# A four-layer vision stack in one kernel: one matmul a half in the chunked scan's preparation, and in the spectral layer fuller matmuls, paired row tiles and five result buffers

## The chip, the cores and the metric

The kernel runs on one core of a Trainium2 chip. The metric is device time in microseconds (us) of that core, the median over the runs. All arithmetic is in float32. A matmul of float32 operands shows in the trace as two records on TensorE (PE), each with its own weight load (PEld); a transpose shows as one. The other engines are DVE (VectorE), ACT (ScalarE), POOL (GpSimd) and SP (SyncE, which here only issues DMAs).

## The reference, cut to what matters

The input is `(8, 64, 64, 96)`: eight images of 64x64 positions and 96 channels. Four layers follow, each a residual step on a group-normed input. Layers 0 and 2 are selective scans over four directions; this change doesn't touch them. Layer 1 is a chunked scan and layer 3 a spectral layer:

```python
x = x + _L1_conv_ref(_gn(x), ...)   # chunked scan: chunks, four directions, decays by exp of sums
x = x + _L3_conv_ref(_gn(x), ...)

# layer 3
xc = jnp.transpose(x, (0, 3, 1, 2))
xu = _upsample_rfft(xc)              # 64x64 -> 128x128, low-passed
h = jnp.transpose(xu, (0, 2, 3, 1))
h = h @ W1.T + b1                    # 96 -> 384
h = coef[:, 0] + coef[:, 1] * h + coef[:, 2] * (h * h)
h = h @ W2.T + b2                    # 384 -> 96
hl = _lpf_rfft(jnp.transpose(h, (0, 3, 1, 2)), cutoff=0.5)
out = hl[:, :, ::2, ::2]             # back to 64x64
return jnp.transpose(out, (0, 2, 3, 1))
```

In layer 1 a projection `x_proj` gives, for each of four directions, 6 step sizes and two vectors of 16 numbers (B and C) at each position.

## The kernel before, in words

The eight images are worked one after the other in a Python loop (`for b in range(batch)`), all unrolled. Within an image each layer is a stage of its own: group norm, `project`, the scan, `back`; the spectral layer closes the image. Where a block says `tc.manual_schedule()` the order of instructions is the one written; elsewhere, and so in both places of this change, a planner orders the instructions of each engine ahead of time by its own costs, and each engine's queue then runs strictly in that order.

**Chunked scan.** `chunked_scan` calls `chunked_order` twice, for `o = 0` (positions by rows) and `o = 1` (by columns), each for two directions `k = o + 2 * i`. The preparation is the first block of `chunked_order`. For `o = 0` it also holds the 3x3 convolution, mostly on DVE (L258), with `silu` on ACT (L272). Then the PE makes B and C for whole rows (`pr`, L782), which DVE copies (`bcs`, L790) and SP sends to DRAM (`bcd`, L793). The loop `for c in range(NQ)` goes over 32 chunks of 128 positions. Each chunk needs its tokens transposed (`xt`, positions on partitions, 192 channels in two halves of 96) and its step sizes and B (`xd`, 2 directions x 22 numbers). For `o = 1` POOL (L802) and ACT (L803) first copy the chunk into rows (`uc`, four buffers). Then come two transposes into `pt` (L807), one copy to `xt` by DVE or ACT in turn (L808), and two matmuls that sum into `px` (L812). `px` takes four chunks and DVE copies it once for the four (L820). After the loop come the step sizes (`dt`, L824, L829), the decays (L834 to L841) and the second block, with its order written by hand, whose first loads (`bt`, `cr`, L863, L867) read `bcd`.

**Spectral layer.** `spectral_layer` is a chain of stages on one image:

- load of `xs` and of the filter matrices `filters` by SP; `xn` by POOL (L1101, 8 blocks);
- 64 transposes to `xt` (L1108), four to a copy by DVE (L1111);
- up-sampling over the rows of the image, 96 matmuls (L1116), one for each channel, whose stationary operand `xt[:, :, c]` has its elements 96 floats apart; 24 copies to `x1`, DVE and ACT in turn (L1121, L1119);
- the main loop, 32 turns of four columns: up-sampling over the columns (L1130, 4 matmuls, 64 rows of the array), copy `x2` by ACT (L1132), three matmuls by `W1` (L1136), each followed by ACT (L1139) and DVE (L1146), 12 matmuls by `W2` (L1153), and the sum into `g` by DVE (L1160);
- down-sampling, 96 matmuls (L1169), one a channel, stationary operand `g[:, :, c]` (elements again 96 floats apart), 64 columns moving; 12 copies to `g2` (L1172, L1174);
- 16 turns of the last filter (L1178) with four transposes of the residual (`p7`, L1181), copy to `res` by ACT (L1185), sum by DVE (L1186), and the DMA out by SP (L1187).

`res` lies in a pool of two buffers. The next image then begins with loads of `tok` (L1217, on SP and on ACT's queue) and transposes (L1223).

Of the kernel before, what the change touches and what calls it, by code (L numbers as in the profile page):

```python
# [17 lines left out]
DM = 96  # L18
# [46 lines left out]
def tile_vision_stack(  # L65
# [678 lines left out]
    def chunked_order(o, w, d, xproj, u, y, yr, cc, lw, bts, bcds, op):  # L744
# [10 lines left out]
        dt = op.tile([128, NQ, 2, RK], F32, name="dt")  # L755
        d_end = op.tile([128, NQ, 2, RK], F32, name="d_end")
        with (
            tc.tile_pool(name="turn", bufs=2) as cp,
            tc.tile_pool(name="pt", bufs=2, space=PSUM) as ptp,
            tc.tile_pool(name="px", bufs=1, space=PSUM) as pxp,  # L760
# [4 lines left out]
            if o == 0:  # L765
                dg = cp.tile([DM, 18, DM], F32, name="dg", bufs=1)
                diagonals(dg, w)
                for rows in ((0, 16), (16, 32), (32, 48), (48, 56)):
                    for hf in range(2):
                        conv(w, y, u, rows, hf)  # L770
                for hf in range(2):
                    acc = acp.tile([DM, 512], F32, name="acc")
                    conv_pe(dg, y, 7, hf, acc)
                    silu(w, u, (56, 64), hf, acc)

# [20 lines left out]
            for c in range(NQ):  # L796
                if o == 0:
                    uv = [u[:, hf, c * Q : (c + 1) * Q] for hf in range(2)]
                else:

                    uc = cp.tile([DM, 2, Q], F32, name="uc", bufs=4)
                    nc.gpsimd.tensor_copy(cut(uc[:, 0, :], True), view(u[:, 0, :], True, c * Q, Q))  # L802
                    nc.scalar.copy(cut(uc[:, 1, :], True), view(u[:, 1, :], True, c * Q, Q))  # L803
                    uv = [uc[:, hf, :] for hf in range(2)]
                pt = ptp.tile([128, 192], F32, name="pt")
                for hf in range(2):
                    nc.tensor.transpose(pt[:, hf * 96 : hf * 96 + 96], uv[hf], ident[:DM, :DM])  # L807
                (nc.vector.tensor_copy if c % 2 else nc.scalar.copy)(xt[:, c, :], pt)  # L808
                if c % 4 == 0:
                    px = pxp.tile([128, 4, 2, RK + NST], F32, name="px")  # L810
                for hf in range(2):
                    nc.tensor.matmul(  # L812
                        px[:, c % 4, :, :],
                        uv[hf],
                        xproj[:, o::2, hf, : RK + NST],
                        start=(hf == 0),
                        stop=(hf == 1),
                    )
                if c % 4 == 3:
                    nc.vector.tensor_copy(xd[:, c - 3 : c + 1, :, :], px)  # L820
# [266 lines left out]
    def spectral_layer(xd, sb, dst):  # L1087

        with tc.tile_pool(name="spec", bufs=1) as lp, tc.tile_pool(name="spec2", bufs=2) as sp:
# [3 lines left out]
            up, down = filters[:64, :128], filters[:, 128:]  # L1093
            xn = lp.tile([DM, L], F32, name="xn")
            xt = lp.tile([64, 64, DM], F32, name="xt", tag="turn")
            x1 = lp.tile([64, 128, DM], F32, name="x1")
            g = lp.tile([128, 128, DM], F32, name="g")
            with tc.tile_pool(name="ps0", bufs=4, space=PSUM) as pp:
# [6 lines left out]
                for h0 in range(0, 64, 4):  # L1105
                    pt = pp.tile([64, 4, DM], F32, name="pt", tag="t")
                    for i in range(4):
                        nc.tensor.transpose(  # L1108
                            pt[:, i, :], xn[:, (h0 + i) * 64 : (h0 + i) * 64 + 64], ident[:DM, :DM]
                        )  # L1110
                    nc.vector.tensor_copy(xt[:, h0 : h0 + 4, :], pt)  # L1111

                for c0 in range(0, DM, 4):
                    pt = pp.tile([64, 4, 128], F32, name="pt", tag="t")
                    for i in range(4):
                        nc.tensor.matmul(pt[:, i, :], xt[:, :, c0 + i], up, start=True, stop=True)  # L1116
                    dv = x1[:, :, c0 : c0 + 4].rearrange("p w c -> p c w")
                    if c0 % 8:
                        nc.scalar.copy(dv, pt)  # L1119
                    else:  # L1120
                        nc.vector.tensor_copy(dv, pt)  # L1121
            with (
# [3 lines left out]
                for w0_ in range(0, 128, 4):  # L1126

                    p2 = pp.tile([DM, 4, 128], F32, name="p2")
                    for i in range(4):
                        nc.tensor.matmul(p2[:, i, :], x1[:, w0_ + i, :], up, start=True, stop=True)  # L1130
# [32 lines left out]
            with tc.tile_pool(name="ps2", bufs=3, space=PSUM) as pp:  # L1163

                g2 = lp.tile([128, 64, DM], F32, name="g2", tag="turn")
                for c0 in range(0, DM, 8):
                    p5 = pp.tile([128, 8, 64], F32, name="p5")
                    for i in range(8):
                        nc.tensor.matmul(p5[:, i, :], g[:, :, c0 + i], down, start=True, stop=True)  # L1169
                    dv = g2[:, :, c0 : c0 + 8].rearrange("p h c -> p c h")  # L1170
                    if c0 % 16:
                        nc.scalar.copy(dv, p5)  # L1172
                    else:
                        nc.vector.tensor_copy(dv, p5)  # L1174

                for h0 in range(0, 64, 4):
# [7 lines left out]
                    res = sp.tile([64, 4, DM], F32, name="res")  # L1184
# [54 lines left out]
def _constants():  # L1239
# [29 lines left out]
    c[:64, K_UP : K_UP + 128] = 2 * low_up[:, ::2].T  # L1269
# [114 lines left out]
```

## Time and profile before

| what | value |
|---|---|
| median of 3 runs | 30100.37 us (30061.18 to 30136.38) |
| the profiled execution, its own time | 30160.23 us |
| its span in the profile | 30158.4 us |
| mean TensorE clock granted in it | 0.754 of full |
| busy: PE, DVE, ACT, POOL | 79%, 82%, 54%, 72% |

The profile lists for each line of the kernel the instructions, their number and mean duration, and what ended the idle time ahead of them. The eight images look alike in it; the times named further on are those of the first image, from the start of the span. A window gives, for a stretch of time, each engine's busy time with the number of records, the granted TensorE clock (1.00 is full) and the DMA's share. A timeline merges like instructions that follow each other: start, length from the first start to the last end, and the number of them.

### The profile page before, as it was taken

To read this page: it belongs to the slowest core of one execution; us is meant where nothing else is said; L and a number is where in the kernel's file an instruction comes from. 1 tells how busy PE (TensorE), PEld (TensorE's weight loads), DVE (VectorE), ACT (ScalarE), POOL (GpSimd) and SP (SyncE) were. 2 spreads that over 40 slices of the span, in tenths; PEclk is the share of its full clock that TensorE was granted. 3 is DMA by queue.
4 is the path that set the end of the run, shared out by engine and by line. 5 is a ranking of instruction groups with operands and counts; after the bars stand their busy time and mean duration, and the time that the engine had idled before them with its cause. 6 is when DMAs were issued, how large, how long until landed. Compare 5 with 4: busy or idle time off the path is not lost. (4 is left out here: it accounts for less than half of the span.)

```text
span 30158.4 us, 279416 instructions
## 1 busy us (share of the span) xinstructions
PE 23685.8 (79%) x90246; PEld 8903.9 (30%) x90246; DVE 24821.0 (82%) x17921; ACT 16367.5 (54%) x28493; POOL 21704.5 (72%) x8844
## 2 busy tenths in 40 slices
PE   7797877978779787797877978779787797877978
PEld 1141412414124141241412414124141241412414
DVE  9879698796987969879698796987969879698796
ACT  5546465464654646546465464654646546465464
POOL 8749487594875948759497594975949759487594
PEclk7687777867768777787777877768777687776877
DMA  5415253152541525415253152531525315253152
GB/s 124 96 35 132 61 124 92 38 131 59 123 94 37 132 58 123 95 37 132 61 123 92 40 132 57 124 92 40 132 58 124 92 39 131 58 124 93 38 132 60
DMA packets 1503971, 2689.40 MB, mean 89 GB/s; under 512 B 305624, under 2 KB 313144, under 8 KB 1502512
## 3 DMA queue, kind: packets, MB, share of 16 engines
q1 hardware_dynamic: 1485872, 2665.23, 37.6%
q8 instruction: 723, 11.85, 0.2%
q10 hardware_dynamic: 16640, 6.29, 0.1%
q14 instruction: 736, 6.03, 0.1%
HBM read 2287.51 MB, written 383.06 MB: 89 GB/s over the span
## 5 line engine op out<-in xcount | busy, mean ns | idle before, releaser
L569 DVE TENSOR_TENSOR_SCAN h<-da,db 128x1026 f32<-128x1026 f32 x6144 | 13729.5, 2281 | 504.0 <-PE py L607 163.8
L590 POOL TENSOR_TENSOR h<-h,c 128x2048 f32<-128x2048 f32 x3072 | 12746.6, 4175 | 146.6 <-ACT state L585 142.4
L533 PE MATMUL pu<-du,cst 32*128 32x512 f32 x4096 | 3240.4, 881 | 3524.5 <-DVE db L539 3499.4
L554 ACT ACTIVATE da<-dx,a0s 128x512 f32<-128x512 f32 x6144 | 4243.4, 691 | 2592.1 <-DVE h L569 2431.3
L554 ACT ACTIVATE da<-dx,a2s 128x512 f32<-128x512 f32 x6144 | 4243.5, 691 | 2589.6 <-DVE h L569 2433.0
L607 PE MATMUL py<-h,cst 128*32 128x512 f32 x24576 | 5415.8, 811 | 68.0 <-POOL h L590 68.0
L539 POOL TENSOR_TENSOR db<-du,b 128x2048 f32<-128x2048 f32 x1024 | 4650.6, 4542 | 580.1 <-ACT db L525 580.1
L539 DVE TENSOR_TENSOR db<-pu,b 128x2048 f32<-128x2048 f32 x2048 | 4642.2, 2267 | 6.3 <-issue 6.3
L607 PEld LDWEIGHTS py<-h,cst 128*32 128x32 f32 x24576 | 1180.7, 145 | 4967.1 <-issue 4529.5
L229 POOL TENSOR_SCALAR xn<-xs,sb 96x512 f32<-96x512 f32 x192 | 203.1, 1062 | 3191.2 <-DVE sb L209 3050.5
L533 PEld LDWEIGHTS pu<-du,cst 32*128 32x128 f32 x4096 | 802.0, 243 | 5542.9 <-DVE db L539 3999.3
L455 PE MATMUL pv<-u,wk 96*128 96x512 f32 x2048 | 1774.1, 1008 | 760.9 <-ACT raw L451 760.9
L446 PE MATMUL pv<-u,wk 96*96 96x512 f32 x2048 | 1480.9, 852 | 515.3 <-ACT state L585 245.0
L597 PE MATMUL py<-y,cst 96*96 96x512 f32 x1536 | 1551.1, 1108 | 403.8 <-ACT raw L460 363.6
L952 ACT ACTIVATE sg<-sg 128x768 f32<-128x768 f32 x1024 | 820.5, 801 | 1400.3 <-PE sg L936 1400.3
L498 POOL TENSOR_TENSOR du<-raw,u 96x512 f32<-96x512 f32 x1024 | 1442.2, 1430 | 0.0
L984 DVE TENSOR_TENSOR wt<-wt,cbm 128x768 f32<-128x768 f32 x1024 | 1022.9, 1004 | 492.1 <-ACT wt L953 491.8
L585 ACT COPY state<-h 128x4 f32<-128x4 f32 x3072 | 607.6, 198 | 1157.3 <-DVE h L569 1157.3
L1146 DVE SCALAR_TENSOR_TENSOR f<-p,w3bs,f 128x512 f32<-128x512 f32 x768 | 576.7, 751 | 719.6 <-ACT f L1139 693.0
L906 POOL TENSOR_TENSOR ce<-ec,cr 96x512 f32<-96x512 f32 x256 | 405.0, 1582 | 976.2 <-ACT ec L904 966.0
L455 PEld LDWEIGHTS pv<-u,wk 96*128 96x128 f32 x2048 | 535.8, 289 | 1921.9 <-ACT raw L451 1444.1
L883 POOL TENSOR_TENSOR rr<-lr,cc 128x768 f32<-128x768 f32 x256 | 375.7, 1468 | 1001.2 <-ACT lr L881 813.5
(210 smaller groups left out, 32525.8 us busy)
## 6 DMA issues: line engine op xcount, KB each, us to landing
dx<-dd SPq DMA_DIRECT2D x4096, 192.0 KB, 3.8
b<-bcd SPq DMA_DIRECT2D x2048, 256.0 KB, 5.2
c<-bcd SPq DMA_DIRECT2D x2048, 256.0 KB, 6.5
du<-dud SPq DMA_DIRECT2D x2048, 128.0 KB, 2.7
dd<-raw SPq DMA_DIRECT2D x1024, 192.0 KB, 5.3
dud<-du SPq DMA_DIRECT2D x512, 128.0 KB, 1.9
xd<-xs SPq DMA_DIRECT2D x256, 192.0 KB, 2.1
xs<-xd SPq DMA_DIRECT2D x128, 384.0 KB, 5.7
```

Of the source, the lines that this page charges most:

```text
L446: nc.tensor.matmul(pv[:DM], weights[k][:, hi, 128:], uv[hi], start=(hi == 0), stop=(hi == 1))
L455: nc.tensor.matmul(pv, weights[k][:, hi, :128], uv[hi], start=(hi == 0), stop=(hi == 1))
L498: nc.gpsimd.tensor_mul(cut(du[:, hf, :], wh), cut(delta[hf], wh), uv[hf])
L533: nc.tensor.matmul(pu, sel[rows, :], m["du"][rows, n // 3, :], start=True, stop=True)
L539: (nc.gpsimd if pool else nc.vector).tensor_mul(groups(m["db", n]), (m["du2"][:, n // 3, :] if pool else m["pu"]) .unsqueeze(1) .to_broadc ...
L554: nc.scalar.activation(dst[:, g, :LC], made[i]["dx"][n // 3][:, n % 3, :], AF.Exp, scale=av4[:, k, n, gs : gs + 1],)
L569: nc.vector.tensor_tensor_scan(made[i]["h", n][:, at][:, way], das[p][:, rev : 2 * SEG + rev][:, way], made[i]["db", n][:, at][:, way], 0. ...
L590: nc.gpsimd.tensor_mul(h, h, made[i]["c"])
L597: nc.tensor.matmul(py, skip[:, hf, :] if k == 0 else ident[:DM, :DM], view((u if k == 0 else y)[:, hf, :], wh, c * LC, LC), start=True, st ...
L607: nc.tensor.matmul(py[32 * q : 32 * q + 32, :], red, hs[q][:, g, :], start=False, stop=(g == NSG - 1),)
L952: nc.scalar.activation(sg, sg, AF.Abs)
L984: nc.vector.tensor_mul(it["wt"], it["wt"], m["cbm"][:, j : j + 1, :].to_broadcast([128, RK, Q]),)
```

## The change

In the preparation the two transposes and two summing matmuls of a chunk become two matmuls, one for each half of the channels. Their moving operand `tx` holds an identity matrix and the projection side by side, 96 + 44 = 140 columns. The result `pt` has both halves' transposed tokens and both halves' share of `xd`; ACT copies the first share and DVE adds the second, for every chunk. `pt` has three buffers and `px` is gone.

In the spectral layer:

- the transposes take 128 columns of `xn` instead of 64 (64 zero columns are added at its end), and `xt` has 128 partitions, of which the filter `up0` weighs the lower half with zeros;
- each result of the row filter is copied by both engines, DVE the first 64 columns and ACT the other 64, so that `x1` holds columns 64 to 127 on partitions 64 to 127;
- the main loop makes the column filter's result for two turns at once: matmuls on rows 0 to 63 and on rows 64 to 127 of the array alternate, into two of three buffers `p2`; the turns go over column groups 0, 64, 4, 68 and so on;
- the down filter is given twice side by side (`down2`, 128 columns moving); only one copy of the result is read, and a buffer holds four channels instead of eight;
- `res` gets a pool of five buffers.

```diff
+        TX = DM + 2 * (RK + NST)
-            tc.tile_pool(name="pt", bufs=2, space=PSUM) as ptp,
-            tc.tile_pool(name="px", bufs=1, space=PSUM) as pxp,
+            tc.tile_pool(name="pt", bufs=3, space=PSUM) as ptp,
...
+            tx = cp.tile([DM, 2, TX], F32, name="tx", bufs=1)
+            for hf in range(2):
+                nc.gpsimd.tensor_copy(tx[:, hf, :DM], ident[:DM, :DM])
+                nc.gpsimd.tensor_copy(
+                    tx[:, hf, DM:].rearrange("p (i r) -> p i r", i=2),
+                    xproj[:, o::2, hf, : RK + NST],
+                )
...
-                pt = ptp.tile([128, 192], F32, name="pt")
+                pt = ptp.tile([128, 2, TX], F32, name="pt")
                 for hf in range(2):
-                    nc.tensor.transpose(pt[:, hf * 96 : hf * 96 + 96], uv[hf], ident[:DM, :DM])
-                (nc.vector.tensor_copy if c % 2 else nc.scalar.copy)(xt[:, c, :], pt)
-                if c % 4 == 0:
-                    px = pxp.tile([128, 4, 2, RK + NST], F32, name="px")
-                for hf in range(2):
-                    nc.tensor.matmul(
-                        px[:, c % 4, :, :],
-                        uv[hf],
-                        xproj[:, o::2, hf, : RK + NST],
-                        start=(hf == 0),
-                        stop=(hf == 1),
-                    )
-                if c % 4 == 3:
-                    nc.vector.tensor_copy(xd[:, c - 3 : c + 1, :, :], px)
+                    nc.tensor.matmul(pt[:, hf, :], uv[hf], tx[:, hf, :], start=True, stop=True)
+                (nc.vector.tensor_copy if c % 2 else nc.scalar.copy)(
+                    xt[:, c, :].rearrange("p (j m) -> p j m", j=2), pt[:, :, :DM]
+                )
+                xdc = xd[:, c, :, :].rearrange("p i r -> p (i r)")
+                nc.scalar.copy(xdc, pt[:, 0, DM:])
+                nc.vector.tensor_add(xdc, xdc, pt[:, 1, DM:])
...
-            up, down = filters[:64, :128], filters[:, 128:]
-            xn = lp.tile([DM, L], F32, name="xn")
-            xt = lp.tile([64, 64, DM], F32, name="xt", tag="turn")
-            x1 = lp.tile([64, 128, DM], F32, name="x1")
+            up, down = filters[:, :128], filters[:, 128:]
+            down2 = lp.tile([128, 2, 64], F32, name="down2")
+            nc.gpsimd.tensor_copy(down2, down.unsqueeze(1).to_broadcast([128, 2, 64]))
+            up0 = lp.tile([128, 128], F32, name="up0")
+            nc.gpsimd.memset(up0[64:], 0.0)
+            nc.gpsimd.tensor_copy(up0[:64], up[:64])
+            xn = lp.tile([DM, L + 64], F32, name="xn")
+            nc.gpsimd.memset(xn[:, L:], 0.0)
+            xt = lp.tile([128, 64, DM], F32, name="xt", tag="turn")
+            x1 = lp.tile([128, 64, DM], F32, name="x1")
...
-                            pt[:, i, :], xn[:, (h0 + i) * 64 : (h0 + i) * 64 + 64], ident[:DM, :DM]
+                            pt[:, i, :], xn[:, (h0 + i) * 64 : (h0 + i) * 64 + 128], ident[:DM, :DM]
...
-                        nc.tensor.matmul(pt[:, i, :], xt[:, :, c0 + i], up, start=True, stop=True)
+                        nc.tensor.matmul(pt[:, i, :], xt[:, :, c0 + i], up0, start=True, stop=True)
...
-                    if c0 % 8:
-                        nc.scalar.copy(dv, pt)
-                    else:
-                        nc.vector.tensor_copy(dv, pt)
+                    nc.vector.tensor_copy(dv[:64], pt[:, :, :64])
+                    nc.scalar.copy(dv[64:], pt[:, :, 64:])
...
-                for w0_ in range(0, 128, 4):
-                    p2 = pp.tile([DM, 4, 128], F32, name="p2")
-                    for i in range(4):
-                        nc.tensor.matmul(p2[:, i, :], x1[:, w0_ + i, :], up, start=True, stop=True)
+                for n in range(32):
+                    w0_ = 4 * (n // 2) + 64 * (n % 2)
+                    if n % 2 == 0:
+                        p2s = [pp.tile([DM, 4, 128], F32, name="p2", bufs=3) for _ in range(2)]
+                        for i in range(4):
+                            for j in range(2):
+                                rows = slice(64 * j, 64 * j + 64)
+                                nc.tensor.matmul(
+                                    p2s[j][:, i, :],
+                                    x1[rows, w0_ + i, :],
+                                    up[rows],
+                                    start=True,
+                                    stop=True,
+                                )
+                    p2 = p2s[n % 2]
...
-                for c0 in range(0, DM, 8):
-                    p5 = pp.tile([128, 8, 64], F32, name="p5")
-                    for i in range(8):
-                        nc.tensor.matmul(p5[:, i, :], g[:, :, c0 + i], down, start=True, stop=True)
-                    dv = g2[:, :, c0 : c0 + 8].rearrange("p h c -> p c h")
-                    if c0 % 16:
-                        nc.scalar.copy(dv, p5)
+                for c0 in range(0, DM, 4):
+                    p5 = pp.tile([128, 4, 2, 64], F32, name="p5")
+                    for i in range(4):
+                        nc.tensor.matmul(
+                            p5[:, i, :, :], g[:, :, c0 + i], down2, start=True, stop=True
+                        )
+                    dv = g2[:, :, c0 : c0 + 4].rearrange("p h c -> p c h")
+                    if c0 % 8:
+                        nc.scalar.copy(dv, p5[:, :, 0, :])
                     else:
-                        nc.vector.tensor_copy(dv, p5)
+                        nc.vector.tensor_copy(dv, p5[:, :, 0, :])
...
-                    res = sp.tile([64, 4, DM], F32, name="res")
+                    res = rp.tile([64, 4, DM], F32, name="res")
...
-    c[:64, K_UP : K_UP + 128] = 2 * low_up[:, ::2].T
+    c[:, K_UP : K_UP + 128] = np.tile(2 * low_up[:, ::2].T, (2, 1))
```

`rp` is the new pool `spec4` with five buffers, opened beside `ps2`.

## The prediction, made before the result was known

> **What bounds the kernel now.** Both places of the change are stages of their own, with nothing of another layer beside them, so I read stages and not the page's shares. The windows of one image come first (start:end, length, then busy us and records of PE, PEld, DVE, ACT, POOL; then granted clock, DMA share, GB/s):
>
> ```profile
> 1488.90:1519.80 30.90, 29.99 (x170) 28.04 (x168) 7.81 (x22) 5.77 (x15) 0.00 (x0) 0.57 0.14 32
> 1748.60:1786.10 37.50, 35.09 (x195) 33.19 (x192) 9.22 (x25) 18.02 (x45) 12.71 (x28) 0.56 0.06 16
> 3490.00:3706.70 216.70, 214.52 (x1214) 154.39 (x1212) 89.94 (x128) 92.58 (x128) 0.00 (x0) 0.98 0.00 1
> 3706.80:3748.60 41.80, 41.76 (x192) 41.79 (x193) 6.11 (x6) 5.12 (x5) 0.00 (x0) 0.52 0.00 1
> 3748.60:3781.10 32.50, 22.35 (x98) 9.19 (x97) 8.73 (x16) 8.38 (x17) 0.00 (x0) 0.87 0.36 88
> ```
>
> The rows are the chunk preparation for o = 0 and for o = 1, the spectral main loop, the down filter, and the output turns. In the first four the PE is the bound: busy 93% or more while no other engine reaches half. In three of those it has half its clock for nearly all the time. The next question is what sets the pace of a record in each; short windows inside the stages tell:
>
> ```profile
> 1489.00:1491.40 2.40, 2.40 (x25) 2.40 (x26) 0.42 (x2) 0.64 (x2) 0.00 (x0) 1.00 0.35 95
> 1500.00:1510.00 10.00, 9.82 (x52) 9.23 (x50) 2.34 (x7) 1.28 (x4) 0.00 (x0) 0.50 0.13 30
> ...
> 3706.90:3708.50 1.60, 1.60 (x8) 1.60 (x8) 0.00 (x0) 0.00 (x0) 0.00 (x0) 1.00 0.00 0
> 3712.00:3713.60 1.60, 1.60 (x9) 1.60 (x9) 0.00 (x0) 0.00 (x0) 0.00 (x0) 0.50 0.00 0
> ```
>
> In the preparation full clock gives a record each 0.096 us and half clock one each 0.192. In the down filter full and half clock give the same: the starts of the records in the trace lie 0.217 us apart in both. So **the clock sets the preparation, and not the down filter**.
>
> For the output turns the timeline shows the wait:
>
> ```profile
> 3755.89 0.47 ACT L1185 COPY res<-p 64x384 f32<-64x384 f32 x1 [0.69 <-DMA out_dram<-res]
> ...
> 3780.02 0.47 ACT L1185 COPY res<-p 64x384 f32<-64x384 f32 x1 [4.16 <-DMA out_dram<-res]
> 3780.52 0.55 DVE L1186 TENSOR_TENSOR res<-res,p 64x384 f32<-64x384 f32 x1 [4.08 <-ACT res L1185]
> ...
> 3781.17 1.06 PE L1223 MATMUL pt<-cst,tok 128*96 128x128 f32 x4 [7.07 <-DVE res L1186]
> ```
>
> ACT waits for an earlier DMA out to free one of two `res`, DVE for ACT, and the next image's first transposes for DVE.
>
> **What the Trainium skill says.** (1) "TensorE: Matmul & The Clock Gate", Part 1: a monitor gates the PE to half clock unless it was busy in a window of about 3.4 us; Part 4 there says that transposes don't count in the same way. The trace agrees: only 1.00 and 0.50 occur, and the preparation falls to 0.50 at 1493.5, some 5 us into it. (2) The same page, Part 3: matmuls on different row groups run at the same time. The trace has such a pair in layer 1 (below). (3) The same page, section on LDWEIGHTS: the load's time goes by columns, not rows. It agrees for contiguous weights (L1153: 128 columns, 0.112 us a record) but not for L1169, 128 columns in 0.217. (4) "SBUF — State Buffer", section "Door 1: The DMA port swizzle", note on cachelines: an access that crosses to a new 16-byte line pays. `g[:, :, c]` steps 384 bytes, `f` in L1153 is contiguous, so this fits; that the stride is the cause no run shows yet.
>
> **Preparation, o = 0.** Removed per chunk: two transposes and two matmuls, six records, 1.22 us at half clock (four chunks take 4.89, e.g. the `xd` copies at 1495.02 and 1499.91) and 0.59 at full. Added: four records of 140 columns. L1130 moves 128 columns in 0.109 us at full clock, so 140 cost 0.117 and 0.233 at half: 0.47 or 0.93 a chunk. The monitor should now see a streaming PE: before, per 0.59 us only 0.15 were matmul streaming (four of 44 columns) and 0.16 transposes.
> Evacuation: the `xt` copy stays (ACT 0.32, DVE 0.36). New are one ACT copy and one DVE sum of 44 columns a chunk; between 192 and 256 columns ACT takes 0.32 and 0.37, DVE 0.34 to 0.36 at 176 and 192, so about 0.20 each for 44. The DVE copy of four chunks (0.34) goes. DVE and ACT then have under 0.4 a chunk: not the bound. But the three users of one `pt` follow each other: 0.74 for the matmuls until the last lands, 0.36 + 0.20 + 0.20, five hand-overs of about 0.04, hence 1.7 us for three buffers, **0.56 a chunk**. It exceeds 0.47, so the PE then waits a little. 29 chunks (three instead of five run ahead during the convolution, while DVE is taken) x 0.56 + 1.1 to fill = 17.3, so the stage ends at 1506.2 instead of 1519.5: **-12.5** with the later end of the chain (0.3) and a little slack. Ends: -7 if half of it stays at half clock, -15. The four POOL copies for `tx` lie in POOL's idle 96 us.
> A queue on SP: `cr` for o = 0 was loaded from 1497.3 under the loop; if its memory now waits for `tx`, it comes after. In o = 1 it already does (1786.2), and from L824 to the first L936 takes 11.2 there and 11.4 in o = 0. So nothing, at most 1 us.
>
> **Preparation, o = 1.** ACT also makes `uc`: for two chunks 2 x 0.50 + 2 x 0.23 + 0.35 with the gaps between = 1.8, 0.90 a chunk; so ACT holds the PE to about half its time, and the clock may fall, which gives 0.93. Either way 32 x 0.93 = 29.8 against 37.5: **-7.5** (ends -3 and -10, by how ACT's strict order stalls).
>
> **Front of the spectral layer.** Transposes of 128 columns: in L807, already with 128, two neighbours lie 0.16 apart at half clock, as in L1108 with 64; free. POOL has five small additions ahead of or between the `xn` blocks, which DVE's 16 copies of 0.55 mostly hide: +0.5 (0 to +3, if `xn` is queued behind the filter's DMA). L1116: 64 strided columns in 0.113 a record, 128 rows change nothing. Each copy is halved over two engines, one after the other on a bank: about 1.2 us per buffer of four, under the 0.9 a group of matmuls needs; the last copy ends 0.5 earlier: **-0.5**.
>
> **Main loop.** L1130 has 8 records a turn, 0.109 each, and the starts show 0.09 more on entering and on leaving it:
>
> ```profile
> 3503.19 1.55 PE L1130 MATMUL p<-filters,x 64*96 64x128 f32 x12
> ...
> 3754.10 0.86 PE L1178 MATMUL p<-g,filters 128*64 128x384 f32 x2
> ...
> 1852.19 1.56 PE L936 MATMUL sg<-rr,lr 32*128 32x384 f32 x8
> ```
>
> L1178 gives 0.32 from one record of 384 columns to the next and 0.54 for the last. Eight of L936 in series would take 7 x 0.32 + 0.54 = 2.8; they take 1.56 since two row groups run together, their weight loads too (starts 7 ns apart). So 16 records for two turns take 8 x 0.109 = 0.87 instead of 1.74: 14 us over 16 pairs. The group is entered 16 times instead of 38, if the planner keeps it whole: up to 4 more. The PE hardly waits (idle 1 us in the loop), and ACT and DVE have 2.9 and 2.8 of 6.6 us a turn. A third `p2` lets a pair start before the last copy `x2`. **-15**, ends -8 (pairs split, waits for `f` show) and -19.
>
> **Down filter.** 96 strided loads of 128 columns, two records each, before and after. 128 moving columns take 0.107 or 0.213, under the 0.217 of the load at either clock. So **0**: 192 x 0.217 = 41.7 stays. 24 copies of half the size lie beside it; the last ends 0.5 earlier, included in 0. Ends -3 and +3; -20 is a rival.
>
> **Output turns.** With five buffers a DMA (2.2 us to land) has 5 x 1.24 us. Then the PE's own pace stays, 1.24 a turn (L1181 at 3753.65, 3754.89, 3756.13). From 3753.65 thirteen turns more end at 3770.2, the last sum at 3771.8 instead of 3781.1. But the loads of `tok` come behind the last PE instruction (3774.1 and 3774.2 now) and need 5 us or so (5.7 landing): the next image starts at about 3776: **-5** (-3 to -7), and -10 at the very end, where no image follows.
>
> **Sum** per image: -12.5 - 7.5 + 0.5 - 0.5 - 15 + 0 - 5 = -40; times 8, and 5 more at the end, -325. The profiled execution would be 30160 - 325 = 29835; it stands 60 above the median, so the median becomes 30100 - 325 = **29775** (-1.1%). A measurement here can tell about 0.3%, 90 us, from no change.
>
> **Rivals.** *A, no pairing and a cold preparation*: row tiles in series, 140 columns at half clock. Gains: 0.29 a chunk for 59 chunks (17), fewer entries (3), output 5; 25 an image, 29900. For: the clock has fallen in every part with waits. Against: L936. *B, the down filter is limited by its low activity*: with wide matmuls 0.112 a record, 20 more, 60 an image: 29620. Against: eight records at clock 1.00 with the same 0.217. *C, slower*: the main loop loses its clock. At half, L1136 goes from 0.43 to 0.85 and L1153 from 0.112 to 0.213, which makes about 5 us more a turn; 160 for the loop. From a quarter of the loop at half clock (40 us) the whole gain is gone; with half of it cold, 80 - 40 = 40 more an image, 30420. For: pairs halve a busy stretch. Against: at 1.00 from 3497.1 to 3708.8, and the streaming of L1136 and L1153 is unchanged.
>
> **Numbers.** Forecast 0.70, A 0.16, B 0.08, C 0.06. The parts' ends summed with care, and most of A, give 29650 to 29910; B and C and a rest lie outside. Faster: forecast, B and most of A, 0.90; same 0.05; slower 0.05.
>
> **What would show it.** Preparation windows at clock 1.00 for o = 0 and about 17 and 30 us long; L1130 in half its time with pairs of equal starts; L1169 still 0.217 a record; no wait of L1185 for a DMA. A down filter of 21 us, or a main loop at a clock of 0.9 or less, would prove me wrong.

## The result, and the profile after

The changed kernel takes **29721.38 us** (median of 4 runs, 29703.03 to 29726.32) against 30086.37 us of the kernel before on the same chip (4 runs, 30061.18 to 30136.38): a ratio of 0.9876, 95% interval 0.9858 to 0.9893. The forecast was 29775, range 29650 to 29910. The profiled execution took 29722.42 us, with a span of 29720.6 us and a mean granted clock of 0.769 (before 30158.4 and 0.754).

The windows of the first image again (start:end, length, then busy us and records of PE, PEld, DVE, ACT, POOL; then granted clock, DMA share, GB/s): chunk loops for o = 0 and o = 1, main loop, down filter, output turns.

```profile
1488.90:1506.50 17.60, 14.66 (x107) 13.22 (x105) 9.54 (x45) 8.06 (x43) 0.00 (x0) 1.00 0.09 22
1731.40:1753.30 21.90, 18.82 (x131) 16.20 (x128) 10.58 (x50) 17.37 (x77) 11.96 (x28) 1.00 0.07 17
3459.60:3668.10 208.50, 199.88 (x1217) 140.92 (x1217) 89.90 (x128) 92.17 (x129) 0.00 (x0) 1.00 0.00 1
3668.10:3710.40 42.30, 42.30 (x193) 42.30 (x194) 7.12 (x12) 6.45 (x11) 0.00 (x0) 1.00 0.00 1
3710.40:3736.70 26.30, 19.81 (x98) 8.07 (x96) 8.74 (x16) 7.98 (x17) 0.00 (x0) 0.96 0.44 103
```

The clock column is what to read first: the stages that stood at 0.52 to 0.57 are at 1.00. (Below, a stage at full clock is called warm and one at half clock cold.) Then the lengths: all are shorter but the down filter, which has the full clock now and takes as long as at half. The short windows inside a stage answer to those shown of before: a preparation with 66 records in 10 us instead of 52, and a down filter with 9 records in 1.6 us, as before.

```profile
1495.00:1505.00 10.00, 8.80 (x66) 8.09 (x65) 4.98 (x24) 4.52 (x25) 0.00 (x0) 1.00 0.01 2
...
3669.00:3670.60 1.60, 1.60 (x9) 1.60 (x9) 0.47 (x1) 0.00 (x0) 0.00 (x0) 1.00 0.00 0
3674.00:3675.60 1.60, 1.60 (x9) 1.60 (x9) 0.24 (x1) 0.19 (x1) 0.00 (x0) 1.00 0.00 0
```

The timeline of the output turns (start, length, then what the engine waited for) has no wait for the DMA out any more. ACT waits 0.77 for the PE's transposes every 1.24 us, and at the end the next image's first transposes wait for the load of their tokens:

```profile
3727.94 0.47 ACT L1209 COPY res<-p 64x384 f32<-64x384 f32 x1 [0.77 <-PE p L1205]
3729.18 0.47 ACT L1209 COPY res<-p 64x384 f32<-64x384 f32 x1 [0.77 <-PE p L1205]
```

```profile
3736.69 1.70 PE L1247 MATMUL pt<-cst,tok 128*96 128x128 f32 x7 [6.31 <-DMA tok<-in_x_dram]
```

By stage, the mean of the eight images, from the traces of both kernels (us; a stage ends where the next one's first instruction starts; the preparation from the first copy of `bcs` to the first sum into `dt`):

| stage | before | after | difference, 8 images | forecast, 8 images |
|---|---|---|---|---|
| preparation, o = 0 | 37.64 | 26.07 | -93 | -100 |
| preparation, o = 1 | 47.47 | 31.57 | -127 | -60 |
| front of the spectral layer | 10.43 | 10.53 | +1 | +4 |
| filter over the rows | 34.29 | 23.23 | -88 | -4 |
| main loop | 217.81 | 208.99 | -71 | -120 |
| down filter | 41.81 | 42.29 | +4 | 0 |
| output turns | 32.84 | 25.85 | -56 | -45 |

The rest of the span makes -8, of which -13 in the scan between the two preparations. The whole is -438 between the two spans; the medians differ by 365, since the profiled execution of before lies 74 above its median and that of after at its own.

Two rows stand out: the filter over the rows, for which nothing was forecast, and the main loop, of which 50 us are missing. The windows of the filter over the rows, of the first and the second image, in the kernel before:

```profile
3466.40:3489.50 23.10, 21.99 (x193) 21.80 (x193) 12.27 (x12) 12.09 (x12) 0.00 (x0) 1.00 0.01 1
7223.20:7264.40 41.20, 40.17 (x192) 39.77 (x192) 12.24 (x12) 12.21 (x12) 0.00 (x0) 0.52 0.00 0
```

and in the kernel after:

```profile
3436.40:3459.70 23.30, 21.96 (x193) 21.80 (x193) 14.00 (x24) 13.88 (x24) 0.00 (x0) 1.00 0.01 1
...
7150.20:7173.40 23.20, 21.92 (x194) 21.73 (x194) 14.00 (x24) 13.88 (x24) 0.00 (x0) 1.00 0.01 1
```

Before, the same stage runs at full clock in three images (23.1 us) and at half in five (40.1 to 41.3). After, all eight take 23.2. So the eight images of the kernel before do not look alike in this stage, as was said of them further up. The forecast was read from the first image, one of the three.

For the main loop, the distances from each record's start to the next one's, credited to the record that begins them (first image, us, with the number of times that the PE leaves such a group):

| record | before | after | order by hand (below) |
|---|---|---|---|
| rows (L1130, after L1142) | 35.3 (38) | 29.2 (26) | 17.6 (16) |
| hidden product (L1136, L1155) | 89.3 | 88.1 | 88.2 |
| output product (L1153, L1172) | 92.7 | 91.1 | 87.4 |

The paired records start 0.006 us apart. From one row record to the next the sum falls from 27.6 to 16.5, so the pairing works. But the step from the last row record to an output product rises from 4.6 us (23 times) to 9.1 (15 times, 0.60 each): it waits. The timeline of the PE (start, length, number, wait ahead) shows for what:

```profile
3521.12 0.90 PE L1142 MATMUL p<-filters,x 64*96 64x128 f32 x12
3522.43 2.47 PE L1172 MATMUL p<-w3bs,f 128*128 128x96 f32 x20 [0.40 <-DVE f L1165]
3524.83 0.46 PE L1142 MATMUL p<-filters,x 64*96 64x128 f32 x2
3525.22 1.12 PE L1155 MATMUL p<-x,w3as 96*128 96x512 f32 x2
```

The rows that stood between `f`'s eviction by DVE and the product that reads `f` have become shorter, and the wait for `f` comes out behind them. A pair is also broken up here: two of its records follow only after 20 records of the output product.

### The profile page after: what moved, and what is told of

Read it like the earlier page. It is cut to its first block, busy times and chain, and to the rows that moved or that the text cites. A ratio compares the mean times of both kernels' runs of the same rounds, so it can differ in the third digit from the quotient of the medians.

```text
span 29720.6 us, 278854 instructions
## 1 busy us (share of the span) xinstructions
PE 23210.2 (78%) x89222; PEld 8452.4 (28%) x89222; DVE 24865.8 (84%) x18449; ACT 16391.5 (55%) x29149; POOL 21705.0 (73%) x8940
## 5 line engine op out<-in xcount | busy, mean ns | idle before, releaser
L229 POOL TENSOR_SCALAR xn<-xs,sb 96x512 f32<-96x512 f32 x192 | 205.2, 1073 | 2995.2 <-DVE sb L209 2538.5
L295 POOL TENSOR_SCALAR xn<-xs,sb 96x512 f32<-96x512 f32 x192 | 146.2, 763 | 1244.5 <-issue 898.9
```

## The experiments

Each is an edit of the kernel after (the first one of the kernel before), run once, the last one four times. The kernel before, run beside them on the same chip, took 30168.59 us for 1 to 4, 30153.23 for 5 to 8, 30151.89 (median of 7) for 9 and 12, and 30096.35 for 10 and 11. Since it moves by that much, the readings rest on the stage means of the traces (us an image, over the eight images).

**1. The preparation alone.** The spectral layer is that of before.

```diff
+ chunked_order as changed
- spectral_layer as changed
+ spectral_layer as before
```

> The kernel before with the change's preparation alone; its spectral layer is that of before. Stages are measured from the first copy of B and C (bcs) to the first addition for dt. If the parts are independent, o = 0 takes 25.9 us an image and o = 1 31.6 as in the changed kernel (37.6 and 47.6 before), 27.5 saved an image, some 220 us in all, and the up filter stays at 23 in some images and 41 in others, mean 34. If the preparation's clock owes something to the spectral edits, o = 0 or o = 1 is longer by several us.

Measured: 29933.66 us. The preparation has its whole gain (26.03 and 31.60); the spectral layer stands as before: row filter 34.43 (41.1 to 41.4 in five images, 23.1 in three), main loop 217.65, down filter 41.79, output 32.93. The two halves of the change add and don't touch each other.

**2. The row filter on 64 rows again**, the wider transposes and split copies kept.

```diff
-    nc.tensor.matmul(pt[:, i, :], xt[:, :, c0 + i], up0, ...)
+    nc.tensor.matmul(pt[:, i, :], xt[:64, :, c0 + i], up[:64], ...)
```

> The changed kernel with the up filter on 64 rows again: stationary operand of 64 rows instead of 128 of which half are multiplied by zeros. Theory: the clock monitor counts how much of the array a matmul fills, so with 64 rows the stage falls to half clock in most images and takes 41 us there (23 at full clock), 5 of 8 images as in the kernel before, some 90 us in all. Rival: the wider transposes ahead of it, which this kernel keeps, are what holds the clock; then it stays at 23 us in all images.

Measured: 29804.13 us, row filter 32.13 us: four images at 40.1 to 41.4 and four at 23.3. The windows of the first two images:

```profile
3435.10:3476.40 41.30, 40.04 (x192) 39.64 (x192) 13.99 (x24) 13.85 (x24) 0.00 (x0) 0.52 0.00 1
7170.60:7193.90 23.30, 22.02 (x194) 21.83 (x194) 13.98 (x24) 13.86 (x24) 0.00 (x0) 1.00 0.00 1
```

The same instructions, once at half and once at full clock. So what the change gained here comes from the 64 further rows of the array, which hold weights of zero, and not from the transposes or the copies. The rows are worth something in the next stage too: the main loop takes 211.26 us instead of 208.99, for it begins cold in seven images here and in two of the changed kernel (at half clock for 3 to 10 us out of its first 13).

With 64 rows, which images are cold can be read from the clock records of the trace. The stretches of one clock are multiples of 3.41 us long, and the clock has always risen in the transposes ahead of the stage. Where it rose 4.00 to 5.63 us ahead of the stage's first matmul, it fell again 6.8 us after the rise and stayed at half to the end of the stage: 14 images. Where it rose 2.81 to 3.94 us ahead, it stayed full: 10 images. That holds for all 24 images with 64 rows (the kernel before, experiment 1 and this one). With 128 rows all 88 images of the changed kernel and of the ten other runs that keep those rows stayed at full clock, rises of over 5 us ahead among them.

**3. Row tiles in series**, in the planner's order.

```diff
-    for i in range(4):
-        for j in range(2):
+    for j in range(2):
+        for i in range(4):
```

> The changed kernel with the two row tiles of a pair one after the other (four matmuls on rows 0 to 63, then four on rows 64 to 127) instead of in turn. Theory: the gain of the main loop is from neighbours on different row groups running together; in series the records are 0.109 us apart again, 11 to 14 us more an image of matmul time, of which 5 to 9 us show in the main loop (208.9 now), since the shorter group exposed waits for f. Rival: the gain is from the cold start that is gone and from fewer entries into the row mode; then the loop stays within 2 us of 208.9.

Measured: 29774.52 us, main loop 212.80, that is 3.8 us an image more, between the theory's 5 to 9 and the rival's 2. In this run the loop begins cold in all eight images, in the changed kernel in two. Between images that were cold for equally long it is 2.1 (213.6 against 211.6, and 212.0 against 209.9), about what the rival allowed; the rest of the 3.8 is clock. The pairing is worth less in this order than its own records say: in the first image the row records take 4.8 us more in series (21.3 against 16.5), and the step from rows to output product, with its wait for `f`, 3.4 less (5.7 against 9.1).

**4. Two result buffers.**

```diff
-    tc.tile_pool(name="spec4", bufs=5) as rp
+    tc.tile_pool(name="spec4", bufs=2) as rp
```

> The changed kernel with two buffers for res again. Theory: the output stage, from the first transpose of the residual to the first transpose of the next image, goes back from 26.5 us to about 33, ACT waits for DMAs out some 20 us an image; 8 x 6.5, about 52 us in all. Rival: part of the stage's gain is from the full clock at its start, which this kernel keeps; then it stops at 31 to 32.

Measured: 29767.92 us, output 31.85. So the buffers are 6.0 of the 7.0 us that this stage gained; 31.85 is what the rival said, and the stage keeps part of its gain without them. The waits of the stage (engine, line, what it waited for: us, times, longest) name the DMA again:

```profile
ACT res L1209 <- DMA out_dram<-res: 16.3, 13, 1.7
DVE res L1210 <- ACT res L1209: 16.2, 14, 1.6
```

**5. to 7. The down filter**: contiguous `g` with 128 moving columns, contiguous with 64, strided with 64.

```diff
-    g = lp.tile([128, 128, DM], F32, name="g")
+    g = lp.tile([128, DM, 128], F32, name="g")
-    nc.tensor.matmul(p5[:, i, :, :], g[:, :, c0 + i], down2, ...)
+    nc.tensor.matmul(p5[:, i, :, :], g[:, c0 + i, :], down2, ...)
```

> The changed kernel with g stored so that the 128 width elements of one channel lie side by side: the down filter's weight loads read a contiguous stationary instead of one with a stride of 384 bytes, and the write of g in the main loop (VectorE, four rows at a time) becomes the strided one. Theory (the stride of the load sets the pace of 0.217 us a record in the down filter): the records fall to about the 0.11 us that contiguous 128-column float32 records of the main loop show, so the stage falls from 42.3 to about 21.5 us an image, unless its evictions (12 a kind) then set it: 22 to 30; the whole falls by about 100 to 165 us. The main loop may grow by up to 5 us an image if the strided write of g takes longer. Rival (evictions, or the product itself, set the pace): the stage stays at 42 and the whole within 20 us of the changed kernel.

> The same contiguous g, and the down filter with the 64 moving columns and eight channels a buffer that the kernel before had. If stride alone sets the pace and the clock would not matter, the stage is about 21.5 us as with 128 columns. Theory: the stage needs both, since with 64 columns the granted clock falls to about half there, as it did before: records of about 0.21 us at half clock in most images, 38 to 42 us. A mixture over the images (some warm, near 22, some cold, near 41) would say that the 64 columns lie at the edge of what holds the clock, as the up filter's 64 rows did.

> The changed kernel with the down filter alone as before: 64 moving columns, eight channels a buffer, strided g. Theory (the strided load sets the pace at either clock): the stage stands at 41.8 us an image instead of 42.3, at a clock of about 0.5, and the output stage that follows begins cold and takes about 1 us more; the whole within 15 us of the changed kernel. Rival (the 128 columns are worth something that the stage's time hides): the whole is slower by 40 us or more.

Measured: contiguous with 128 columns 29557.73 us, the stage 21.51 in every image; contiguous with 64 columns 29601.34, mean 27.99: five images at 21.5 and three at 38.6 to 39.4; strided with 64 columns 29725.35, 41.78 (clock 0.52 to 0.55), and the output stage 27.42 instead of 25.85. The first two kernels' windows (128 columns; then 64 columns, first and second image):

```profile
3672.60:3694.10 21.50, 21.50 (x193) 21.50 (x194) 7.27 (x12) 6.68 (x11) 0.00 (x0) 1.00 0.01 2
```

```profile
3671.10:3692.60 21.50, 21.48 (x193) 21.50 (x194) 6.31 (x6) 5.16 (x5) 0.00 (x0) 1.00 0.01 2
7359.30:7398.70 39.40, 39.40 (x193) 39.40 (x194) 6.24 (x6) 5.06 (x5) 0.00 (x0) 0.52 0.00 0
```

The stride of the weight load is the cause of 0.22 us a record (42.29 / 192): without it a record takes 21.51 / 192 = 0.112. The main loop, which now writes `g` with a stride, stays at 209.05. With the stride gone, the doubled columns that the change brought begin to count: with them the clock held in all images, with 64 columns in five of eight; why in those five, the record does not show. In the changed kernel itself they are worth only the warm start of the stage that follows, 1.6 us an image, less the 0.5 that they cost.

**8. Two buffers for the preparation's result.**

```diff
-    tc.tile_pool(name="pt", bufs=3, space=PSUM) as ptp
+    tc.tile_pool(name="pt", bufs=2, space=PSUM) as ptp
```

> The changed kernel with two result buffers of the name pt instead of three. Theory (in the preparation the matmul of a half waits for the copy that frees the buffer before last, and three are just what the copies' latency needs): the first kind of preparation goes from 0.625 to about 0.85 us a chunk, 7 to 10 us an image more, the second kind about 5 us more; other users of pt (tokens, transposes) some us more: the whole 100 to 200 us slower. Rival (ScalarE's and VectorE's own work sets the pace, buffers don't): both stages within 2 us an image.

Measured: 29834.86 us; 32.30 for o = 0 (+6.2) and 40.09 for o = 1 (+8.5; 38.8 to 39.1 in the six images at a clock of 1.00, 43.5 and 43.9 in the two at 0.77). The chain of a buffer's users sets the pace, as the forecast had it; the size is a little less than expected for o = 0 and more for o = 1.

**9. and 10. The main loop's order by hand**, with the rows in pairs, and with the rows in series.

```diff
+    tc.manual_schedule(),
...
+    for n in range(32):
+        if n < 31:
+            hidden(n + 1)
+        if n < 30:
+            if n % 2 == 0:
+                rows(n + 2)     # the pair n + 2 and n + 3
+            narrow(n + 2)       # the copy x2
+        output(n)
```

> The changed kernel with the main loop's order written by hand in place of the planner's: step by step the hidden product of tile n+1, then (every other tile) the paired rows of tiles n+2 and n+3 and the copy of tile n+2, then the output product of tile n, so that a hidden product of some 2.5 us stands between f's eviction and the output product that reads it. Theory (about 7 us an image of what the pairing saved is lost to the wait for f, which comes from the order): the main loop falls from 209 to 190 to 200 us an image, the waits of the output product for VectorE's f nearly go, and the whole falls by 70 to 150 us. Rival (TensorE's own work fills the loop, the wait for f only takes the place of other idle time, or ScalarE and VectorE set the pace): the loop stays within 4 us of 209 or grows, the whole within 30 us or slower.

> The main loop's order by hand with the row transforms one tile after the other instead of in pairs on the two halves of the array. It gives the price of the pairing where no wait for f stands beside it. Theory (pairing is worth what the row matmuls' own records show, 27.6 us less 16.5, and 2.5 us of fewer turns of the array's shape, and with the planner's order it is partly covered by the wait for f): the main loop goes from 192 to 203 to 207 us an image, 11 to 14 more than with pairs, and the whole to about 29,660 to 29,690. Rival (the loop by hand is set by ScalarE or VectorE, so that the pairing matters no more than in the planner's order): the main loop is 4 us an image longer or less.

Measured: in pairs 29575.86 us, main loop 191.92 us, 17 less than in the planner's order; in series 29636.55 us, main loop 198.85. The PE's timeline of the first:

```profile
3513.04 2.77 PE L1160 MATMUL p<-x,w3as 96*128 96x512 f32 x6
3515.74 1.12 PE L1142 MATMUL p<-filters,x 64*96 64x128 f32 x16
3516.79 2.92 PE L1180 MATMUL p<-w3bs,f 128*128 128x96 f32 x24
3519.54 2.77 PE L1160 MATMUL p<-x,w3as 96*128 96x512 f32 x6
3522.15 2.82 PE L1180 MATMUL p<-w3bs,f 128*128 128x96 f32 x24
```

No wait is left in this stretch, and every group is whole: the pair is 16 records in 1.12 us, and the group of rows is left 16 times an image instead of 26. The wait for `f` was thus a matter of order. The 17 us are more than the 7 that the expectation had put on the wait. In the first image it is 15.3: of the 11.7 in the row records (table above), 6.1 are the step to an output product that no longer waits, 2.9 lie between row records, since pairs stay whole, and 2.7 in the steps from rows to the hidden product, 1 instead of 11; 3.7 lie in the output product, which the PE leaves 31 times instead of 79. In this image the loop by hand begins cold (clock 0.98 over the loop) and that of the planner does not. In the third image, where both are at 1.00, it is 18.5; the further 3.1 are in the hidden product (85.0 against 88.1).

The run in series met neither expectation: pairs are worth 6.9 us in the order by hand, between the theory's 11 to 14 and the rival's 4 (7.7 between images that were cold for equally long). The trace gives the reason. In series, the records start 0.109 us apart at both ends of the sixteen, but in the middle 0.026 and 0.083 by turns, as if the second tile's, on the other half of the array, ran beside the first tile's. The sum from row record to row record is 27.6 before, 21.8 in this series and 13.6 in pairs. Against the rows of before, all on one half, pairs thus save 14.0, the forecast's figure; part of it comes with the two halves alone.

**11. ScalarE relieved in the second preparation.**

```diff
-    (nc.vector.tensor_copy if c % 2 else nc.scalar.copy)(xt...
+    (nc.vector.tensor_copy if o or c % 2 else nc.scalar.copy)(xt...
```

> The changed kernel with all 32 of the preparation's copies of the transposed half for the second kind on VectorE, none on ScalarE: 16 copies of about 0.3 us an image fewer for ScalarE. It tests the step of the forecast that had ScalarE's summed durations set the pace of the second kind. Theory (ScalarE's copies overlap, and it isn't what sets the pace): the second kind's preparation stays within 2 us of 31.6 us an image or grows by up to 4 as VectorE gets the copies. Rival (ScalarE sets it): it falls by about 16 x 0.3 = 5 us an image, 40 us in the whole.

Measured: 29767.23 us; the stage grew by 6.7 us to 38.32: 34.6 in four images (clock 1.00), 38.5 in one (0.85), and 43.1 in three (0.69). The rival's 5 us did not come. At full clock the growth is 3.0, within the theory's bound of 4: all copies in VectorE's queue lengthen the chain that frees `pt` (0.75 us a chunk in the timeline instead of 0.64). That the clock falls in the other four images the theory did not have. As the edit moves the work into that very chain, it shows that less work for ACT alone gains nothing, not how near ACT is to its own limit.

**12. The version that beats both**: the order by hand and the contiguous `g` together.

> The order by hand together with the contiguous g for the down filter (128 columns). Theory: the two gains lie in different stages and add: 70 to 150 us of the main loop and what the contiguous g alone gave (about 165 us against the changed kernel): about 29,450 us, against before a ratio of about 0.979. Rival: VectorE's strided write of g is in the way of the shorter loop, so that the sum is 50 us or more short of the two parts.

Measured over 4 runs: **29414.84 us** (29409.81 to 29420.23), beside before 30151.89 (7 runs): ratio 0.9757, interval 0.9741 to 0.9774. Main loop 191.18 and down filter 21.51: the gains add. VectorE's strided write of `g` raises its busy time in the loop (89.95 to 98.12 us of 193, first image) and costs nothing that shows, for VectorE is idle for about half of the loop.

## Why the prediction was right, and where it was not

The forecast's case came, the time 54 us below it and within the range. That the sum is so near is in part luck: it has two errors of opposite sign, 50 us too much for the main loop and some 150 too little for the second preparation and the row filter. The profiled execution itself came out 113 us below its forecast (29722 against 30160 - 325 = 29835). The median is nearer because the forecast took off the 60 us by which the profiled execution of before stood above its median, and that of after stands at its own.

- **Preparation, o = 0: right.** Clock 1.00, and four chunks take 2.50 us, 0.625 a chunk against 0.56; -11.6 an image against -12.5. Experiment 8 shows the chain of `pt` that the step was built on. The gain is the clock and not the smaller number of records: the prediction's window at full clock has 25 records in 2.40 us, so the six records of a chunk took 0.58 us there, less than the 0.625 of now. Experiment 1 shows that the new preparation holds the clock by itself. Whether that comes from matmuls in the place of transposes or from 140 moving columns instead of 44, no run separates.
- **Preparation, o = 1: the step undersized the gain, -15.9 against -7.5.** The failed term is "0.90 a chunk" for ACT. It added durations that overlap, and took some of them too long. ACT's lines of two chunks in the timeline of the changed kernel show it:

```profile
1741.62 0.32 ACT L816 COPY xt<-pt 128x192 f32<-128x192 f32 x1
1741.83 0.29 ACT L820 COPY xd<-pt 128x44 f32<-128x44 f32 x2
1742.00 0.80 ACT L810 COPY uc<-u 96x128 f32<-96x128 f32 x2
```

  The copy of `xd` starts 0.21 after the start of a copy of 0.32, and a second one adds 0.09 to the first's 0.20; a pair of `uc` takes 0.80, not the 2 x 0.50 assumed. The Trainium skill, "ScalarE: Activation LUTs", section "What ACT_TABLE_LOAD costs", states that back-to-back ACTIVATEs overlap by about 93 ns; the 0.11 here agrees, and the step should have used it. So two chunks take 1.28 us on average and not 1.8, the PE was not held to half its time, and the clock stayed. At 0.64 a chunk ACT and PE are both busy about 89% (4.56 and 4.53 of 5.10 us in a window of eight chunks), and they wait for each other in turn; which of them would bound it alone stays open.
- **Row filter: the step "128 rows change nothing: -0.5" failed, -11.1.** Records do follow each other at 0.113 to 0.114 at full clock with 64 and with 128 rows, but the clock was not full in five images of eight. Two errors made it: one image was taken for eight, and rows were taken to matter for the load only. Experiment 2 settles the cause. The copies did not matter, as forecast (DVE and ACT busy 14.0 and 13.9 of 23.3 us), though the prediction's sentence on them calls 1.2 us less than 0.9.
- **Main loop: the mechanism right, the size too large, -8.8 against -15.** The pairs came at the price forecast where nothing stands in their way, 14 us by the records (27.6 to 13.6 in the order by hand); in the planner's order the records show 11.1 (27.6 to 16.5). The end "-8, pairs split, waits for `f` show" is what happened, and experiment 9 shows both parts by taking them away. The forecast took the middle without asking what the PE does between `f`'s eviction and its use when the rows no longer fill that time; the waits for `f` of the kernel before, 7.9 us of the weight loads and 1.0 of the matmuls, were the warning. And part of the -8.8 is none of the pairs' doing. The loop began cold in all eight images before (0.98) and after the change in two (0.98 and 0.99, with 211.6 and 209.9 us against 208.4 in the six others). From the mean of before to the image that was cold about as long it is -6.2, outside the forecast's ends; the other 2.6 are a warm start, most of which experiment 2 loses again with the 64 rows (211.26).
- **Down filter: right.** 0.22 a record at full clock in the same stage, and experiment 5 shows the stride to be the cause, which the prediction left open. Rival B fell: the clock did rise to 1.00 and the stage took 42.3.
- **Output turns: right**, -7.0 against -5. The 6.0 of the buffers were the term; the rest fits the stage's start at full clock (experiment 7: 1.6 us), which the forecast had not carried on from the down filter.
- **Rivals A and C fell.** Pairs start together, the preparation is warm, and the main loop's clock is 1.00 in six images and no lower than 0.98 in the others. What a cold start of the loop costs shows within the changed kernel: the hidden product takes 91.2 us in the second image, which began cold, and 88.1 in the first.

The kernel before spreads over 75 us in its runs and the changed one over 23. Five cold row filters at 18 us each, sometimes more and sometimes fewer, would make such a spread; that is an estimate from the two durations of the stage, and no run shows it.

## What to carry to other kernels

Read every repetition of a stage before costing an edit at nothing: a stage that is warm in one image and cold in the next gives a difference that no instruction explains. When an edit shortens work on the bounding engine, ask which wait that work was covering, and keep in the order by hand something of the length of the eviction between a product and the one that reads it. A pace that didn't change with the clock pointed to an operand's layout here, and a strided stationary operand is worth moving the stride to an engine that has time.

## What the runs showed of the hardware

- In these runs the granted clock went with how much of the array was at work and not only with how long the PE was busy. The PE was busy 40.17 of 41.20 us in the row filter of the second image and had a clock of 0.52. With 64 rows and 128 moving columns this stage was cold in 14 of 24 images; with 128 rows, half of them zeros, in none of 88. In the down filter with contiguous weights 64 moving columns were cold in three of eight images, 128 in none of 16 (experiments 5 and 12). In the preparation the windows of 10 us have the PE busy 9.82 us at a clock of 0.50 before and 8.80 us at 1.00 after. The Trainium skill, "TensorE: Matmul & The Clock Gate", Part 1, speaks of how busy the PE has been; here two streams equally busy in time were treated differently, and the measurement decides.
- After its first 3 us the row filter with 64 rows kept the clock that it had then: a full clock stayed full for the other 20 us of the stage, and a half clock stayed at half for some 38 (experiment 2).
- Records whose weight load has 128 columns with a stride of 384 bytes follow each other at about 0.22 us at either clock (the down filter before, 41.81 us at half, and after, 42.29 at full, for 192 records); with contiguous weights and full clock at 0.112.
- Two tiles on the two halves of the rows overlap in part even if their matmuls are issued one tile after the other: 21.8 us an image from row record to row record against 27.6 on one half, and 13.6 when they alternate.
